# A decoder layer's layernorms: reciprocal roots by a power on GpSimd in place of ScalarE's root and VectorE's reciprocal

## The chip, the cores and the metric

The kernel runs on one core of a Trainium2 chip. A core has five engines with a queue each: TensorE (PE in the profile; PEld are its weight loads), VectorE (DVE), ScalarE (ACT), GpSimd (POOL) and SyncE (SP), which here only issues DMAs. Each engine works its queue in order; semaphores order them among each other. The metric is the device time of one execution in microseconds (us); lower is better.

## The reference

One transformer decoder layer in float32 on x of 4 batches x 1024 tokens x 256 features, with a context of 64 tokens for each batch:

```python
x = x + self_attention(layernorm(x))            # 16 heads of 16, scores not scaled
x = x + cross_attention(layernorm(x), context)  # 16 heads of 16
x = x + ffn(layernorm(x))
# layernorm(v) = (v - mean(v)) / sqrt(var(v) + 1e-5), over the last axis
# ffn(v): h = gelu(v @ ternary(W_fc).T)          # 256 -> 1024
#         h = layernorm(h) * ln_w + ln_b
#         h @ ternary(W_proj).T                  # 1024 -> 256
```

So each batch goes through four layernorms: three over the 256 features of x, and one over the 1024 features inside the feed-forward network (FFN).

## The kernel before

Tokens lie on the 128 partitions; a batch is 8 tiles of 128 tokens. The work has three stretches.

**Start (to about 60 us).** The first batch's layernorm (`ln1(0)`), its projections and loads. Here `state["pinned"]` is true: VectorE's layernorm instructions are held in the order in which the program gives them.

**Attention loop (about 60 to 1090 us).** 16 units (4 batches x 4 head groups) of 16 steps. A step computes scores (TensorE, with the row maxima subtracted by a matmul on `sel`), four exps of 128x512 on ScalarE (L911), the row maxima of the next unit on VectorE (`mx`, L449), and eight weighing matmuls into `ps_acc`. PSUM banks come from a ring of seven. Everything else is written as generators that yield between pieces, and three lines (`due`, `later`, `aside`) with credits decide at which step a piece is put in: the next batches' first layernorm, projections and values; for a finished batch `post(b)`, that is its output projection, the second layernorm, the whole cross-attention, and the statistics of the third layernorm, whose results are kept in `mv3` and `rs3` until the FFN needs them.

**FFN (from about 1087 us).** Eight halves of 512 tokens. `widen(i)` normalises x, multiplies by W_fc, applies Gelu (L1031) and takes the statistics of h (L1034, L1035); after the fourth tile it takes the reciprocal root (`ln_rstd`), then normalises h (VectorE L1042, ScalarE L1045, two tiles each). `narrow(i)` transposes h, splits it into `hT` (ScalarE, L1065) and `hl` (VectorE, L1066) and multiplies by W_proj. The pieces of the wide and narrow halves and of the last batch's `post(3)` are interleaved by a list of places (`WIDE`, `NARROW`) and by tags that a generator yields ("Gelu", "Sqrt", "free Exp").

**A layernorm's steps.** `ln_stats` gives mean and variance of each tile (`mv`; VectorE, L241 and L242). `ln_rstd` makes 1/sqrt(var + eps) for 4 or 8 tiles at once: a root on ScalarE (`sd`, L247) and a reciprocal on VectorE (`rs`, L248). `ln_normalised`, in the attention loop, makes `nmr` = -mean x rs on VectorE (L254) and then eight ScalarE instructions of 128x256 (`xn`, L258); outside it works on VectorE (L265). In the FFN `nmr` is L1039.

**What sets the order.** The matmuls, transposes and SyncE's DMAs are held in program order. The other instructions of VectorE, ScalarE and GpSimd are placed by the framework's scheduler, by its own estimate of when each will be ready; once placed, a queue runs in that order and an instruction that waits holds up what stands behind it. ScalarE's functions come from a table that is loaded by an instruction of its own (ACT_TABLE_LOAD), which the compiler puts in where the function needs another table; the root's, Exp's and Gelu's tables differ, and plain copies and Identity need no load.

GpSimd does little after the start: the copies that pack `xwk` and `xwq` for the cross-attention (L479), two widening copies (L545, L777), and the additions of the output biases to x in the attention loop (`add_row`, L291).

Of the kernel before, what the change touches and what calls it, by code (L numbers as in the profile page):

```python
# [9 lines left out]
F32 = mybir.dt.float32  # L10
F32R = mybir.dt.float32r
DRAM = bass.MemoryType.DRAM
AF = mybir.ActivationFunctionType
ALU = mybir.AluOpType
# [7 lines left out]
P = 128  # L22
NT = S // P
NG = 4
NU = B * NG
LN_EPS = 1e-5
# [4 lines left out]
def decoder_layer(ctx, tc, a, out):  # L31
# [15 lines left out]
    nc = tc.nc  # L47

    const = ctx.enter_context(tc.tile_pool(name="const", bufs=1))
    main_stack = ExitStack()  # L50
    main = main_stack.enter_context(tc.tile_pool(name="main", bufs=1))


    ordered = tc.keep_in_program_order

    def matmul(*args, **kwargs):
        ordered(nc.tensor.matmul(*args, **kwargs))  # L57
# [55 lines left out]
    for name in ("bq", "bk"):  # L113

        t = const.tile([P, 2], F32, name=f"{name}_c")
        for g in range(NG):
            r = 64 * (g % 2)
            dma(
                out=t[r : r + 64, g // 2 : g // 2 + 1],
                in_=a[name].rearrange("(j e) g -> g j e", e=32)[g, :, 1 : 1 + D],  # L120
# [5 lines left out]
    make_identity(nc, ident)  # L126
    eps_t = const.tile([P, 1], F32, name="eps_t")
    nc.vector.memset(eps_t, LN_EPS)

    kx = const.tile([P, 2, B, 4, SK], F32, name="kx")  # L130
    vx = const.tile([P, B, H // 2, 2, 32], F32, name="vx")
# [4 lines left out]
    mv3 = const.tile([P, B * NT, 2], F32, name="mv3")  # L136
    rs3 = const.tile([P, B * NT], F32, name="rs3")
# [6 lines left out]
    post_pool = post_stack.enter_context(tc.tile_pool(name="post", bufs=1, side="right"))  # L144
# [38 lines left out]
    state = {"split": False, "banks": "ring", "pinned": True}  # L183

    def pinned(ins):

        if state["pinned"]:
            ordered(ins)
# [48 lines left out]
    def ln_stats(pool, mv, blocks):  # L237

        for i, t in blocks:
            st = pool.tile([P, 6], F32, tag="bn", name="bn", bufs=3)  # L240
            pinned(nc.vector.bn_stats(out=st, in_=xs(t)[:, 0, :]))  # L241
            pinned(nc.vector.bn_aggr(out=mv[:, i, :], in_=st))  # L242

    def ln_rstd(pool, rs, mv):
        n = mv.shape[1]
        sd = pool.tile([P, n], F32, tag="sd", name="sd", bufs=2)
        nc.scalar.activation(sd, mv[:, :, 1], AF.Sqrt, bias=eps_t[:, 0:1])  # L247
        pinned(nc.vector.reciprocal(out=rs, in_=sd))  # L248

    def ln_normalised(pool, mv, rs, i, t, n):  # L250
        xn = pool.tile([P, n, E], F32, tag="xn", name="xn", bufs=2)
        if state["split"]:
            nmr = pool.tile([P, n], F32, tag="nmr", name="nmr", bufs=2)
            nc.vector.scalar_tensor_tensor(  # L254
                nmr, mv[:, i : i + n, 0], -1.0, rs[:, i : i + n], ALU.mult, ALU.mult
            )
            for k in range(n):
                nc.scalar.activation(  # L258
                    xn[:, k, :], xs(t + k)[:, 0, :], AF.Identity, bias=nmr[:, k : k + 1],
                    scale=rs[:, i + k : i + k + 1],  # L260
                )
            return xn
        for k in range(n):
            pinned(
                nc.vector.tensor_scalar(  # L265
                    xn[:, k, :], xs(t + k)[:, 0, :], mv[:, i + k, 0:1], rs[:, i + k : i + k + 1],
                    ALU.subtract, ALU.mult,
                )
            )
        return xn  # L270
# [64 lines left out]
    def ln1(b):  # L335
        mv = main.tile([P, NT, 2], F32, tag="mv1", name="mv1", bufs=2)
        rs = main.tile([P, NT], F32, tag="rs1", name="rs1", bufs=2)
        xnT_of[b] = xnT = main.tile([P, 2, S], F32, tag="xnT", name="xnT")
        n = NT if state["split"] else NT // 2
        for i0 in range(0, NT, n):  # L340
            for i in range(i0, i0 + n, 2):
                yield "free"
                ln_stats(main, mv, [(i + k, b * NT + i + k) for k in range(2)])
            yield "free"
            ln_rstd(main, rs[:, i0 : i0 + n], mv[:, i0 : i0 + n, :])
            for i in range(i0, i0 + n, 4):
                yield "free"
                xn = ln_normalised(post_pool, mv, rs, i, b * NT + i, 4)
                yield "rows"
                ln_transposed(xnT[:, :, i * P : (i + 4) * P], xn)  # L350
# [205 lines left out]
    def post(b):  # L556
# [15 lines left out]
        mv = post_pool.tile([P, NT, 2], F32, tag="mv2", name="mv2")  # L572
        rs = post_pool.tile([P, NT], F32, tag="rs2", name="rs2")
        for i in range(0, NT, 2):
            yield "free"
            ln_stats(post_pool, mv, [(i + n, t0 + i + n) for n in range(2)])
        yield "free Sqrt"
        ln_rstd(post_pool, rs, mv)
        for half in range(2):
            h0 = half * 4  # L580
            xnT = post_pool.tile([P, 2, 512], F32, tag="xn2T", name="xn2T")
# [76 lines left out]
        sl = slice(t0, t0 + NT)  # L658
        for i in range(0, NT, 2):
            yield "free"  # L660
            ln_stats(post_pool, mv3[:, sl, :], [(i + n, t0 + i + n) for n in range(2)])
        yield "free Sqrt"
        ln_rstd(post_pool, rs3[:, sl], mv3[:, sl, :])
        if b < B - 1:
            dma(out=x_kept[:, sl, :], in_=x_of[b])

# [247 lines left out]
    for u in range(NU):  # L914
# [27 lines left out]
        for step in range(2 * NT):  # L942
# [16 lines left out]
            exps = [scores(u, half, kb, 0)]  # L959
# [42 lines left out]
    ffn = ctx.enter_context(tc.tile_pool(name="ffn", bufs=1))  # L1002
# [4 lines left out]
    def widen(i):  # L1007
        t0 = i * NH
        xh = ffn.tile([P, 2, NH * P], F32R, tag="xh", name="xh", bufs=2)
        xl = ffn.tile([P, 2, NH * P], F32R, tag="xl", name="xl", bufs=2)  # L1010
        for t in range(0, NH, 2):
            cols = slice(t * P, (t + 2) * P)
            xn = ln_normalised(ffn, mv3, rs3, t0 + t, t0 + t, 2)
            ln_transposed(xh[:, :, cols], xn, rest=xl[:, :, cols])
            if t == 0:
                yield ""
        h = ffn.tile([P, NH, HID], F32, tag="h", name="h", bufs=2)
        mv = ffn.tile([P, NH, 2], F32, tag="mvh", name="mvh", bufs=2)
        rs = ffn.tile([P, NH], F32, tag="rsh", name="rsh", bufs=2)
        h_of[i] = h  # L1020
        for t in range(NH):
            yield "Gelu"
            ph = ps["wide"]()
            for half in range(2):
                for k in range(4):
                    c, part = divmod(k, 2)
                    matmul(
                        ph[:, half, :], lhsT=(xl, xh)[part][:, c, t * P : (t + 1) * P],
                        rhs=wfc[:, c, half * 512 : (half + 1) * 512], start=k == 0, stop=k == 3,
                    )  # L1030
            nc.scalar.activation(h[:, t, :], ph.rearrange("p a f -> p (a f)"), AF.Gelu)  # L1031
            st = ffn.tile([P, 2, 6], F32, tag="bnh", name="bnh", bufs=3)
            for half in range(2):
                nc.vector.bn_stats(out=st[:, half, :], in_=h[:, t, half * 512 : (half + 1) * 512])  # L1034
            nc.vector.bn_aggr(out=mv[:, t, :], in_=st)  # L1035
        yield "Sqrt"
        ln_rstd(ffn, rs, mv)
        nmr = ffn.tile([P, NH], F32, tag="nmr", name="nmr", bufs=2)
        nc.vector.scalar_tensor_tensor(nmr, mv[:, :, 0], -1.0, rs, ALU.mult, ALU.mult)  # L1039
        for t in range(0, NH, 2):  # L1040
            yield ""
            nc.vector.tensor_scalar(  # L1042
                h[:, t, :], h[:, t, :], mv[:, t, 0:1], rs[:, t : t + 1], ALU.subtract, ALU.mult
            )
            nc.scalar.activation(  # L1045
                h[:, t + 1, :], h[:, t + 1, :], AF.Identity, bias=nmr[:, t + 1 : t + 2],
                scale=rs[:, t + 1 : t + 2],
            )
# [62 lines left out]
    wides = [Source(widen(i), 16 * i, WIDE) for i in range(halves)]  # L1111
    narrows = [Source(narrow(i), 16 * (i + 1), NARROW) for i in range(halves)]
    exps = turn = 0
    tag = later.tag
    while tag is not None or narrows:
        turn += 1
        if tag is not None and turn % 5 in (0, 2):
            exps += "Exp" in tag
            tag = next(last, None)
            continue  # L1120
        sources = []
        if wides:
            i = halves - len(wides)
            first = len(wides[0].places) <= len(WIDE) - 2
            late_x = i >= 2 * (B - 1) and tag is not None
            full = first and len(narrows) > halves + 1 - i
            apart = exps % NG and tag is not None and wides[0].tag in ("Gelu", "Sqrt")
            if not (late_x or full or apart):
                sources.append(wides[0])
        if narrows and len(narrows) > len(wides):  # L1130
            sources.append(narrows[0])
        if not sources:
            continue
        source = min(sources, key=lambda source: source.places[0])
        source.step()
        if not source:
            (wides if source in wides else narrows).pop(0)
# [58 lines left out]
```

## Time and profile before

| | us |
|---|---|
| three runs | 1352.6, 1344.46, 1348.62 |
| their median | 1348.62 |
| span of the profiled execution, first to last instruction | 1348.4 |
| TensorE, weight loads, VectorE busy | 1277.8, 718.3, 1012.5 |
| ScalarE, GpSimd busy | 896.7, 57.3 |
| mean granted TensorE clock | 0.983 |

The page gives no other time of the profiled execution than its span, which lies 0.2 us below the median. The profile counts as busy what an engine executes; the ends of matmuls are modelled, so a busy TensorE may also be one that goes slowly. A group's line gives the line of the program, engine, operation, output and inputs, shapes and count, then busy time in us and the mean of one in ns, then the idle time just before and who ended it. A timeline's line starts with the start and the duration in us; an idle time before it and its releaser stand in brackets. Granted clock is 1 at full speed and 0.5 when halved.

### The profile page before, as it was taken

What the parts mean: (1) busy time and instruction counts of PE and PEld (TensorE: products, weight loads), DVE (VectorE), ACT (ScalarE), POOL (GpSimd) and SP (SyncE); (2) the same over time, 40 slices, a digit from 0 to 9 for tenths busy, and PEclk for the clock granted to TensorE, in tenths of its full rate; (3) what the DMA queues carried; (4) which work ended last, traced back from release to release, by engine and by line L of the source; (5) the groups of instructions that cost most, each with busy time, mean ns of one, the idle gap of its engine ahead of it and who ended that gap; (6) DMA issues with size and microseconds to landing.
All of it is one profiled execution on the core that took longest, in us unless ns stands there. A gap on an engine that the chain in (4) does not pass through costs nothing.

```text
span 1348.4 us, 27671 instructions
## 1 busy us (share of the span) xinstructions
PE 1277.8 (95%) x11000; PEld 718.3 (53%) x11000; DVE 1012.5 (75%) x2130; ACT 896.7 (67%) x1654; POOL 57.3 (4%) x74
## 2 busy tenths in 40 slices
PE   4889999999999999999999999999999999999887
PEld 2445444545554454444545544545455467676777
DVE  5888877767877877788877777878889369584765
ACT  2377776666677667777676676686766756565854
POOL 5000000021010000011000000010000000000000
PEclk9889999999999999999999999999999999999989
DMA  5442321302020211221111102212210020200000
GB/s 170 122 135 66 93 74 54 96 32 80 33 79 1 64 28 36 70 57 44 53 48 49 44 21 79 80 55 71 55 41 1 1 64 0 64 0 32 1 32 32
DMA packets 46577, 72.73 MB, mean 54 GB/s; under 512 B 11536, under 2 KB 28176, under 8 KB 46448
## 3 DMA queue, kind: packets, MB, share of 16 engines
q1 hardware_dynamic: 45232, 68.73, 17.0%
q8 instruction: 87, 1.43, 0.4%
q0 software_dynamic: 400, 0.66, 0.3%
q10 hardware_dynamic: 816, 1.57, 0.3%
q14 instruction: 42, 0.34, 0.1%
HBM read 46.81 MB, written 24.12 MB: 53 GB/s over the span
## 4 chain that ended last, share of the span: by engine, by line
PE 73%; DVE 16%; ACT 7%; DMA 2%; issue 1%; DVEq 0%; ACTq 0%; SPq 0%
PE ps_ring L57 42%; PE ps_acc L57 15%; PE ps_wide L57 8%; DVE mx L449 8%; PE ps_misc L57 3%; DVE nm L605 3%; PE ps_misc L60 3%; ACT exp L911 2%; PE ps_ring L60 2%; ACT xn L258 1%; DVE bn L241 1%; DVE xn L265 1%; DMA x<-in_x 1%; ACT ex L638 1%; DMA kept_q<-hl 1%
## 5 line engine op out<-in xcount | busy, mean ns | idle before, releaser
L449 DVE TENSOR_REDUCE mx<-ps_ring 128x1 f32<-128x512 f32 x1024 | 645.9, 681 | 151.3 <-PE ps_ring L57 150.5
L911 ACT ACTIVATE exp<-ps_ring 128x512 f32<-128x512 f32 x1024 | 549.1, 607 | 180.5 <-PE ps_ring L57 177.1
L57 PE MATMUL ps_ring<-q,k 64*128 64x512 f32 x1024 | 280.0, 475 | 6.7 <-ACT exp L911 5.9
L57 PE MATMUL ps_ring<-k,q 64*128 64x512 f32 x1024 | 263.3, 423 | 16.1 <-DMA k<-kept_k 6.9
L57 PE MATMUL ps_acc<-exp,v_sb 128*32 128x512 f32 x2048 | 274.5, 608 | 0.0
L57 PE MATMUL ps_ring<-mT,sel 64*128 64x512 f32 x1024 | 233.1, 401 | 0.2 <-ACT mT L467 0.2
L57 PEld LDWEIGHTS ps_ring<-q,k 64*128 64x128 f32 x1024 | 115.9, 186 | 197.1 <-ACT exp L911 68.4
L57 PEld LDWEIGHTS ps_ring<-k,q 64*128 64x128 f32 x1024 | 125.6, 186 | 96.6 <-ACT exp L911 42.1
L57 PEld LDWEIGHTS ps_ring<-mT,sel 64*128 64x128 f32 x1024 | 108.4, 187 | 6.4 <-ACT mT L467 0.7
L57 PEld LDWEIGHTS ps_acc<-exp,v_sb 128*32 128x32 f32 x2048 | 40.4, 108 | 67.4 <-issue 65.6
L1066 DVE SCALAR_TENSOR_TENSOR hl<-ps_misc,lnw,hT 128x512 fp32r<-128x512 f32 x64 | 46.6, 733 | 20.0 <-ACT hT L1065 19.8
L1034 DVE BATCH_NORM_STATS2 bnh<-h 128x6 f32<-128x512 f32 x64 | 41.1, 679 | 24.8 <-ACT h L1031 24.8
L57 PE MATMUL ps_wide<-wfc,xl 128*128 128x512 f32 x128 | 56.2, 439 | 3.4 <-DVE xl L281 2.9
L1031 ACT ACTIVATE h<-ps_wide 128x1024 f32<-128x1024 f32 x32 | 32.7, 1025 | 36.9 <-PE ps_wide L57 36.9
L57 PE MATMUL ps_wide<-wproj,hl 128*128 128x256 f32 x256 | 46.7, 305 | 10.6 <-DVE hl L1066 10.5
L57 PE MATMUL ps_wide<-wfc,xh 128*128 128x512 f32 x128 | 53.1, 415 | 0.0
L1065 ACT ACTIVATE hT<-ps_misc,lnw 128x512 fp32r<-128x512 f32 x64 | 42.9, 687 | 15.4 <-PE ps_misc L60 15.3
L241 DVE BATCH_NORM_STATS2 bn<-x 128x6 f32<-128x256 f32 x96 | 38.9, 416 | 6.0 <-DMA x<-in_x 4.3
L57 PEld LDWEIGHTS ps_wide<-wproj,hl 128*128 128x128 f32 x256 | 35.3, 194 | 14.3 <-DVE hl L1066 12.6
L57 PE MATMUL ps_wide<-wproj,hT 128*128 128x256 f32 x256 | 41.9, 287 | 0.0
L421 ACT COPY v_sb<-ps_ring 128x256 f32<-128x256 f32 x32 | 12.1, 377 | 40.1 <-PE ps_ring L57 40.1
L60 PE MATMUL ps_misc<-ident,h 128*128 128x128 f32 x256 | 37.5, 276 | 0.0
(168 smaller groups left out, 1430.1 us busy)
## 6 DMA issues: line engine op xcount, KB each, us to landing
q<-kept_q SPq DMA_DIRECT2D x240, 64.0 KB
k<-kept_k SPq DMA_DIRECT2D x240, 64.0 KB
kept_q<-hl SPq DMA_DIRECT2D x15, 512.0 KB
kept_k<-hl SPq DMA_DIRECT2D x14, 512.0 KB
out<-x SPq DMA_DIRECT2D x16, 256.0 KB
x<-in_x SPq DMA_DIRECT2D x3, 1024.0 KB
x_kept<-x SPq DMA_DIRECT2D x3, 1024.0 KB
x<-x_kept SPq DMA_DIRECT2D x3, 1024.0 KB
```

Source lines behind the costliest of these rows:

```text
L57: ordered(nc.tensor.matmul(*args, **kwargs))
L60: ordered(nc.tensor.transpose(*args))
L241: pinned(nc.vector.bn_stats(out=st, in_=xs(t)[:, 0, :]))
L258: nc.scalar.activation(xn[:, k, :], xs(t + k)[:, 0, :], AF.Identity, bias=nmr[:, k : k + 1], scale=rs[:, i + k : i + k + 1],)
L265: nc.vector.tensor_scalar(xn[:, k, :], xs(t + k)[:, 0, :], mv[:, i + k, 0:1], rs[:, i + k : i + k + 1], ALU.subtract, ALU.mult,)
L449: nc.vector.tensor_reduce(mx[:, t, 2 * pair + n : 2 * pair + n + 1, kh], pm, AX.X, ALU.max)
L605: nc.vector.tensor_reduce(nm[:, t, s, :], pm[s].rearrange("p (h k) -> p h k", k=SK), AX.X, ALU.max, negate=True,)
L911: nc.scalar.activation(ex[:, n, :], pe[n], AF.Exp)
L1031: nc.scalar.activation(h[:, t, :], ph.rearrange("p a f -> p (a f)"), AF.Gelu)
L1034: nc.vector.bn_stats(out=st[:, half, :], in_=h[:, t, half * 512 : (half + 1) * 512])
L1065: nc.scalar.activation(hT, pt, AF.Copy, scale=w)
L1066: nc.vector.scalar_tensor_tensor(hl, pt, w, hT.bitcast(F32), ALU.mult, ALU.subtract)
```

## The change

The reciprocal root of all layernorms but the first batch's first one goes to GpSimd, as two instructions: rs = var + eps, and rs = rs to the power of -0.5, the exponent read from a constant column (`minus_half`) that VectorE sets once at the start. The first batch's keeps the root and the reciprocal. The tag "Sqrt", by which the pieces around a root were placed, is gone: `fill` looks only for "free", "rows", "cols" and "Exp", so the first two of its uses change no order by themselves; the third one is in the FFN's test `apart`, which now holds back only pieces tagged "Gelu".

```diff
+    minus_half = const.tile([P, 1], F32, name="minus_half")
+    nc.vector.memset(minus_half, -0.5)
...
-    def ln_rstd(pool, rs, mv):
+    def ln_rstd(rs, mv):
         n = mv.shape[1]
-        sd = pool.tile([P, n], F32, tag="sd", name="sd", bufs=2)
-        nc.scalar.activation(sd, mv[:, :, 1], AF.Sqrt, bias=eps_t[:, 0:1])
-        pinned(nc.vector.reciprocal(out=rs, in_=sd))
+        if state["pinned"]:
+            sd = main.tile([P, n], F32, tag="sd", name="sd", bufs=2)
+            nc.scalar.activation(sd, mv[:, :, 1], AF.Sqrt, bias=eps_t[:, 0:1])
+            ordered(nc.vector.reciprocal(out=rs, in_=sd))
+            return
+        nc.gpsimd.tensor_scalar(rs, mv[:, :, 1], LN_EPS, None, ALU.add)
+        nc.gpsimd.tensor_tensor(rs, rs, minus_half[:, 0:1].to_broadcast([P, n]), ALU.pow)
...
-        yield "free Sqrt"
-        ln_rstd(post_pool, rs, mv)
+        yield "free"
+        ln_rstd(rs, mv)
...
-        yield "free Sqrt"
-        ln_rstd(post_pool, rs3[:, sl], mv3[:, sl, :])
+        yield "free"
+        ln_rstd(rs3[:, sl], mv3[:, sl, :])
...
-        yield "Sqrt"
-        ln_rstd(ffn, rs, mv)
+        yield ""
+        ln_rstd(rs, mv)
...
-            apart = exps % NG and tag is not None and wides[0].tag in ("Gelu", "Sqrt")
+            apart = exps % NG and tag is not None and wides[0].tag == "Gelu"
```

More of the change, by code (lines that the diff above doesn't have):

```diff
@@ L344, in ln1 @@
             yield "free"
-            ln_rstd(main, rs[:, i0 : i0 + n], mv[:, i0 : i0 + n, :])
+            ln_rstd(rs[:, i0 : i0 + n], mv[:, i0 : i0 + n, :])
             for i in range(i0, i0 + n, 4):
```

## The prediction

> **What bounds the kernel now.** I read the page from its first two parts to the groups, then the timeline around every table load.
>
> ```profile
> PE 1277.8 (95%) x11000; PEld 718.3 (53%) x11000; DVE 1012.5 (75%) x2130; ACT 896.7 (67%) x1654; POOL 57.3 (4%) x74
> ...
> PEclk9889999999999999999999999999999999999989
> ```
>
> TensorE is busy 95% of the span, so what ScalarE and VectorE do counts only where TensorE waits for them. GpSimd has 57 us of work: it has room.
>
> ```profile
> L247 ACT ACT_TABLE_LOAD x19 | 24.4, 1283 | 1.1 <-PEq L1185 0.7
> ...
> L1031 ACT ACT_TABLE_LOAD x12 | 15.4, 1283 | 2.0 <-PE ps_wide L57 1.8
> ...
> L911 ACT ACT_TABLE_LOAD x9 | 11.5, 1283 | 0.8 <-PE ps_ring L57 0.6
> ...
> L291 POOL TENSOR_TENSOR x<-x,bo 128x512 f32<-128x512 f32 x16 | 20.0, 1280 | 239.4 <-DVE nmr L254 207.9 <-DVE bo L551 27.7 <-ACT xn L258 3.8
> ```
>
> These groups (split by shape) show 43 table loads of 1283 ns with three more at L638. ScalarE's function table goes to the root's and back to Exp's or Gelu's around nearly every layernorm. Now what one costs in the attention loop: ScalarE's timeline at the second layernorm of batch 0.
>
> ```profile
> 362.28 1.28 ACT L247 ACT_TABLE_LOAD   x1
> 363.58 0.30 ACT L247 ACTIVATE sd<-mv,eps_t 128x8 f32<-128x8 f32 x1
> 363.90 1.28 ACT L911 ACT_TABLE_LOAD   x1
> 365.19 2.06 ACT L911 ACTIVATE exp<-ps_ring 128x512 f32<-128x512 f32 x4
> ```
>
> ScalarE gives no exp for 2.9 us. What TensorE loses by it is read from its own timeline: each step of the loop ends in eight weighing matmuls,
>
> ```profile
> 363.86 1.07 PE L57 MATMUL ps_acc<-exp,v_sb 128*32 128x512 f32 x8
> ...
> 368.61 1.06 PE L57 MATMUL ps_acc<-exp,v_sb 128*32 128x512 f32 x8
> ```
>
> and steps with the same matmuls can be compared, since undisturbed ones repeat to 0.02 us. The step between these two lasts 4.75; the same matmuls elsewhere (from 110.04) take 3.77. From 358.93 on, four steps last 4.93, 4.75, 3.37 and 5.38 us, and undisturbed 4.62, 3.77, 2.89 and 4.25: 2.9 us lost. I did this for each root in the loop. Lost: first layernorm of batch 1 (at 80 us) 7.4, of batch 2 (161) 1.9, of batch 3 (580) 4.0; second of batches 0, 1, 2 (362, 621, 886) 2.9, 2.8, 2.9; third of batches 0, 1 (564, 832) 1.7 and 1.5. Together 25 us, and not all the table's: eight normalisations of 0.5 us each also stand on ScalarE among the exps.
>
> **What the change removes.** In the built programs' orders ScalarE has 43 table loads before and 9 after: it loses 34 (18 before a root, 16 that went back) and 19 roots: 34 x 1.283 + 19 x 0.30 = 49 us. VectorE loses 19 reciprocals of 0.2 us, 4 us. TensorE's and SyncE's instructions stand in the same order as before. The Trainium skill, "ScalarE: Activation LUTs", section "What ACT_TABLE_LOAD costs", adds a drain of about 1380 ns to each switch, 2.66 us in all; by it ScalarE would be freed of 96 us. The trace disagrees: an exp ends at 161.11, the load starts at 161.13, the root at 162.43, so I use 1.283.
>
> **What it adds.** GpSimd gets 19 additions and 19 powers, 11 pairs on 128x8 and 8 on 128x4. No row shows a power. From below: the add of 128x512 takes 1.28 us, a memset of 128x1 0.10, so eight columns at an add's price come to 0.10 + 8 x 1.18/512 = 0.12 us. From above: the whole 128x512 add, 1.28 us, which is 64 additions' worth for each element; more than that I can't exclude and keep as a rival. I take the upper end, 1.28 (and 0.7 for four columns), because a logarithm and an exponential in a chain are nearer to many additions than to one. Adding 0.12 for the addition and some 0.25 for three handoffs (VectorE to ScalarE took 0.04 at 83.93), the way from the last statistics to the root is L = 1.65 us for 128x8 and 1.1 for 128x4. Before, it was 0.56 at best (83.93 to 84.49), and up to 2.7 behind a load.
>
> The new wait stands on VectorE: in the loop the scaled mean (nmr, L254) now follows the last aggregate directly or nearly so, so VectorE stands still for L, and the maxima (L449) and bias splits (L371) behind it free PSUM banks late. On ScalarE the first normalisations stand ahead of the next exps and wait too.
>
> **Attention loop, term by term.**
> - Third layernorms of batches 0 and 1: nobody needs the root for long, so all of it goes: 1.7 + 1.5 = **+3.2 us**.
> - Second layernorms (three): ScalarE waits for the root from 362.26 to about 363.9 instead of standing in loads to 365.19, 1.3 us less; but VectorE waits 1.65 it did not wait before, and the normalisations now come in a denser bunch (three and two between pairs of exps). I take 0.9 each: **+2.7**.
> - First layernorm of batch 2: **+0.7** of 1.9; of batch 3: ScalarE gets to its normalisations at 581.3 instead of 583.75, **+1.7** of 4.0.
> - First layernorm of batch 1: **-3.0**. There the load lay beside VectorE's statistics (ScalarE waited until 83.96 anyway), so nothing is won. And GpSimd's queue has a new order: the addition and the power stand ahead of the eight copies of xwk (L479). These ran at 78.82 and TensorE took them at 80.27; now they wait for the statistics' end (83.93) + 1.65 + eight copies at 0.19 = 87.1. TensorE, in order, stands from 80.2 to 87.1 instead of from 82.7 to 86.7, and kx (L518) and the maxima behind it on VectorE come some 4 us later. Against that the load back to Exp (88.29) goes: net -3.
>
> Sum of the loop: **5.3 us**.
>
> **The FFN's end.** From 1087 us on, eight halves each end in a root that their normalisation (L1042, L1045) waits for. From last statistics to first use: 2.5, 1.45, 3.1, 2.9, 2.2, 3.2, 1.35, 1.35 us; after, about 1.35 each. It counts where TensorE stands: 2.9 us at 1114, 1.5 at 1254, 2.7 at 1279, 2.9 at 1303, 1.5 at 1328. Take 1303, on ScalarE's timeline, then TensorE's:
>
> ```profile
> 1300.05 1.28 ACT L247 ACT_TABLE_LOAD   x1
> 1301.34 0.30 ACT L247 ACTIVATE sd<-mvh,eps_t 128x4 f32<-128x4 f32 x1
> 1301.55 0.57 ACT L279 CAST xh<-ps_misc 128x512 fp32r<-128x512 f32 x1
> 1302.08 2.37 ACT L1045 ACTIVATE h<-h,nmr,rsh 128x1024 f32<-128x1024 f32 x2
> ```
>
> ```profile
> 1306.36 1.01 PE L57 MATMUL ps_wide<-wproj,hl 128*128 128x256 f32 x3 [2.89 <-DVE hl L1066]
> ```
>
> Here statistics end at 1300.62 and the root comes as late as before; only the two transposed copies (xh) now stand where the load stood, which brings hT and so TensorE's wproj forward 0.6 us. The same reading gives 1.15 at 1114, 0.85 at 1254, 1.85 at 1279, 1.0 at 1328: 5.45 us. A window of 14 us shows a second price (the granted clock is the third number from the right, 0.76):
>
> ```profile
> 1300.00:1314.00 14.00, 11.11 (x57) 9.62 (x55) 7.31 (x14) 7.79 (x10) 0.00 (x0) 0.76 0.11 39
> ```
>
> After such a gap the clock is halved, here for 6.8 us, 3.4 us after the gaps at 1114 and 1279. Half of these 13.6 us is lost. "TensorE: Matmul & The Clock Gate", section "HAM oscillation", of the Trainium skill puts the limit at idle gaps over about 3.4 us; by it nothing would be won back here. The trace throttles after 2.7 to 2.9. I count one window of 3.4 us avoided, 1.7. Loads back to Gelu lie in waits for TensorE (5.07 us at 1311.88) and bring nothing. Sum: **7.2 us**.
>
> **Sum:** 5.3 + 7.2 = 12.5 from the span of 1348.4: 1336 us. The span and the median of the runs (1348.6) agree, so 1336 it is.
>
> **Rivals.**
> 1. *The power is slow and VectorE stands behind it* (slower). Each us more of L costs six loop layernorms 1 us each and five halves about 0.5: 8.5 us. The gain is used up when the power of 128x8 takes 1.28 + 12.5/8.5 = 2.75 us; at 5 us the time is 1336 + 31 = 1367. For: no row bounds it. Against: GpSimd's rows are short, and VectorE is idle 25% of the time. The skill's "GPSIMD Engine Reference", section 2.1, has about 6 us for the first call of newly loaded code; no run here shows it; by it the layernorm at 80 us would lose 6 more, 1342.
> 2. *The loads were hidden* (no change): new order and bunched normalisations give back what the loads took, the clock windows stay, batch 1 loses more: 1346.
> 3. *Larger gain:* power near its lower end (L 0.5: 8.5 x 1.15 = 10 us more) and all clock windows gone: 1322.
> That all 34 loads go is fixed by the program and is no open point.
>
> **Chances.** A measurement here tells 0.5%, 6.7 us, from no change. Forecast (1328 to 1341) 0.45; larger gain 0.15; no change 0.2; slow power 0.2. So faster 0.6, same 0.2, slower 0.2. The range takes in the lower bound of the power and part of rival 1: 1321 to 1358; in my own case 1328 to 1341.
>
> **What would show it.** Right: 9 table loads on ScalarE; steps at the third layernorms of batches 0 and 1 at their undisturbed length; GpSimd's power near 1.3 us; VectorE idle before L254 about 1.6 us, released by GpSimd; TensorE idle near 80 to 87 us on xwk. Wrong: powers over 2.75 us; TensorE idle in the FFN's halves no shorter; more windows of halved clock than now.

## The result, and the profile after

The changed kernel takes **1364.38 us** (median of four runs, 1363.3 to 1365.78); the kernel before, on the same chip, 1348.54 (1344.46 to 1352.6). The ratio is 1.0116, 95% interval 1.01 to 1.0132: some 16 us slower, where 12.5 us faster was forecast. The profiled execution's span is 1362.7 us, 14.3 more than before.

The head of the page and the slices of TensorE's granted clock, of after:

```profile
PE 1279.9 (94%) x11000; PEld 722.2 (53%) x11000; DVE 1009.2 (74%) x2112; ACT 850.5 (62%) x1601; POOL 89.1 (7%) x112
...
PEclk9889999999999999999999999999999999998989
```

What was to go has gone: ScalarE is busy 46.2 us less (896.7 to 850.5) with 53 instructions fewer (34 loads and 19 roots), VectorE 3.3 us less, and 9 table loads are left. TensorE executes the same 11000 matmuls and is busy 2.1 us more; the other 12 us of the longer span are idle time of TensorE. Now the price that no row of before had, the groups on GpSimd by shape, in the trace of after (count, then busy us and ns of one):

```profile
L254 POOL TENSOR_TENSOR rs<-rs,minus_half 128x8 f32<-128x8 f32 x11 | 18.3, 1666 | 0.9
...
L254 POOL TENSOR_TENSOR rsh<-rsh,minus_half 128x4 f32<-128x4 f32 x8 | 8.3, 1037 | 0.7
```

The power on 128x8 takes 1.67 us, not 1.28, and on 128x4 1.04, not 0.7. Only 0.4 us each: that doesn't explain 28 us between forecast and result.

**Where the time went, in the attention loop.** Steps with the same matmuls were compared, as in the prediction (before to after, lost is plus): first layernorm of batch 1 +0.9, of batch 2 +2.7, of batch 3 -2.1; second layernorms +1.1, +0.6 and +1.1; third layernorm of batch 0 -1.6 and then +2.4, of batch 1 -1.5. With small changes elsewhere the loop is about 3 us longer. Look at one second layernorm, that of batch 0, on VectorE's timeline (start, duration, engine, line, operation; in brackets the idle time before and who ended it). Before:

```profile
361.84 0.18 DVE L242 BATCH_NORM_AGGREGATE mv<-bn 128x2 f32<-128x6 f32 x1
362.30 0.48 DVE L371 SCALAR_TENSOR_TENSOR hl<-ps_ring,bk_c,hl 128x256 f32<-128x256 f32 x1 [0.27 <-ACT hl L370]
362.70 1.28 DVE L449 TENSOR_REDUCE mx<-ps_ring 128x1 f32<-128x512 f32 x2
363.91 0.20 DVE L248 RECIPROCAL rs<-sd 128x8 f32<-128x8 f32 x1
364.03 1.24 DVE L449 TENSOR_REDUCE mx<-ps_ring 128x1 f32<-128x512 f32 x2
365.18 0.22 DVE L254 SCALAR_TENSOR_TENSOR nmr<-mv,rs 128x4 f32<-128x4 f32 x2
```

and after:

```profile
365.56 0.18 DVE L244 BATCH_NORM_AGGREGATE mv<-bn 128x2 f32<-128x6 f32 x1
367.85 0.23 DVE L260 SCALAR_TENSOR_TENSOR nmr<-mv,rs 128x4 f32<-128x4 f32 x2 [2.11 <-POOL rs L254]
368.00 0.48 DVE L377 SCALAR_TENSOR_TENSOR hl<-ps_ring,bk_c,hl 128x256 f32<-128x256 f32 x1
368.39 2.47 DVE L455 TENSOR_REDUCE mx<-ps_ring 128x1 f32<-128x512 f32 x4
```

Before, VectorE split the bias (hl) and took two maxima while ScalarE loaded its table and took the root, and two more before nmr. After, nmr stands first, VectorE does nothing for 2.11 us, and the same hl and the maxima come behind it. What TensorE makes of it, on its timeline of after:

```profile
366.41 0.40 PE L57 MATMUL ps_ring<-mT,sel 64*128 64x512 f32 x2
368.53 0.49 PE L57 MATMUL ps_ring<-k,q 64*128 64x512 f32 x1 [1.73 <-DVE hl L377]
```

TensorE needs a PSUM bank that hl has to read first, and stands for 1.73 us. A second price follows in after's windows of 4 us (the third number from the right is the granted clock, the first is TensorE's busy time):

```profile
366.00:370.00 4.00, 2.12 (x14) 0.84 (x14) 2.15 (x6) 1.96 (x5) 1.73 (x2) 1.00 0.15 60
370.00:374.00 4.00, 4.00 (x32) 1.91 (x26) 1.35 (x3) 3.59 (x9) 2.61 (x3) 0.57 0.20 75
```

In the four us after the gap the mean granted clock is 0.57. The second layernorm of batch 1 allows an estimate of what this adds. TensorE has the same gap there, and the clock stays at 1.00:

```profile
626.52 0.50 PE L57 MATMUL ps_ring<-k,q 64*128 64x512 f32 x1 [1.75 <-DVE hl L377]
628.00:632.00 4.00, 3.43 (x36) 1.65 (x28) 1.93 (x5) 4.00 (x10) 3.11 (x3) 1.00 0.00 0
```

The loss is 0.6 us here and 1.1 for batches 0 and 2, whose gap is followed by a halved window: some 0.5 us for each such window, in this place. (In the last run below, e14, all three gaps are followed by a halved window, and the three lose alike, 2.0 to 2.2 us.) In all, the clock is halved during 64 us of after's execution and 46 of before's. The 18 us between them are five such windows of 3.4 us, so an estimate from these three layernorms is 2 to 3 us in all, and half of 18, 9, is the most that they can cost.

**In the FFN** after is a further 11 us behind. One place of it, after's timeline (some lines left out):

```profile
1185.87 0.15 DVE L1041 BATCH_NORM_AGGREGATE mvh<-bnh 128x2 f32<-128x12 f32 x1
...
1186.13 1.07 ACT L285 CAST xh<-ps_misc 128x512 fp32r<-128x512 f32 x2 [1.18 <-PE ps_misc L60]
...
1187.57 0.16 DVE L1045 SCALAR_TENSOR_TENSOR nmr<-mvh,rsh 128x4 f32<-128x4 f32 x1 [1.16 <-POOL rsh L254]
1187.65 1.53 DVE L1048 TENSOR_SCALAR h<-h,mvh,rsh 128x1024 f32<-128x1024 f32 x2
...
1189.10 1.28 DVE L287 TENSOR_TENSOR xl<-ps_misc,xh 128x512 fp32r<-128x512 f32 x2
1189.84 0.51 PE L57 MATMUL ps_wide<-wfc,xl 128*128 128x512 f32 x1 [2.43 <-DVE xl L287]
```

The same instructions before, on VectorE:

```profile
1181.30 0.15 DVE L1035 BATCH_NORM_AGGREGATE mvh<-bnh 128x2 f32<-128x12 f32 x1
...
1182.18 0.69 DVE L281 TENSOR_TENSOR xl<-ps_misc,xh 128x512 fp32r<-128x512 f32 x1
...
1184.48 0.15 DVE L1039 SCALAR_TENSOR_TENSOR nmr<-mvh,rsh 128x4 f32<-128x4 f32 x1
1184.55 1.53 DVE L1042 TENSOR_SCALAR h<-h,mvh,rsh 128x1024 f32<-128x1024 f32 x2
```

TensorE waits for xl, the low part of the next half's input. Before, the first xl came 0.7 us behind the aggregate and the normalisation of h followed 2.4 us later, when the root was there. After, nmr and the 1.53 us of h stand ahead of xl, which comes 3.1 us behind the aggregate; TensorE falls 2.3 us further back here. The same pattern returns with attx in xl's place (at 1267, 2.2 us) and, at 1285, with hl: there the wait is that of the last batch's third layernorm, whose normalisation (xn, on VectorE in this stretch) stands ahead of statistics and of the split that TensorE needs:

```profile
1282.99 0.41 DVE L271 TENSOR_SCALAR xn<-x,mv,rs 128x256 f32<-128x256 f32 x1 [2.12 <-POOL rs L254]
1283.32 1.28 DVE L1040 BATCH_NORM_STATS2 bnh<-h 128x6 f32<-128x512 f32 x2
1284.52 0.73 DVE L1072 SCALAR_TENSOR_TENSOR hl<-ps_misc,lnw,hT 128x512 fp32r<-128x512 f32 x1
```

In sum, the waits of VectorE for the power (total us, times, longest), after:

```profile
DVE nmr L260 <- POOL rs L254: 10.9, 6, 2.1
DVE nmr L1045 <- POOL rsh L254: 8.8, 8, 1.5
DVE xn L271 <- POOL rs L254: 4.0, 2, 2.1
```

23.7 us, where VectorE waited 7.0 us for ScalarE's roots before (4.2 for `rs`, 2.8 for `rsh`), beside a span that is 14.3 us longer.

### The profile page after: what moved, and what is told of

Same layout as the page of the kernel before. It is cut to its first block, busy times and chain, and to the rows that moved or that the text cites. A ratio compares the mean times of both kernels' runs of the same rounds, so it can differ in the third digit from the quotient of the medians.

```text
span 1362.7 us, 27635 instructions
## 1 busy us (share of the span) xinstructions
PE 1279.9 (94%) x11000; PEld 722.2 (53%) x11000; DVE 1009.2 (74%) x2112; ACT 850.5 (62%) x1601; POOL 89.1 (7%) x112
## 4 chain that ended last, share of the span: by engine, by line
PE 74%; DVE 18%; ACT 4%; POOL 2%; DMA 2%; issue 1%; POOLq 0%; SPq 0%; DVEq 0%; ACTq 0%
PE ps_ring L57 44%; PE ps_acc L57 16%; DVE mx L455 7%; PE ps_wide L57 7%; DVE nm L611 3%; PE ps_ring L60 2%; PE ps_misc L57 2%; PE ps_misc L60 2%; ACT exp L917 1%; DVE bnh L1040 1%; DVE bn L243 1%; DVE hl L1072 1%; POOL rs L254 1%; DVE xn L271 1%; ACT h L1037 1%
## 5 line engine op out<-in xcount | busy, mean ns | idle before, releaser
L57 PE MATMUL ps_ring<-q,k 64*128 64x512 f32 x1024 | 277.0, 474 | 1.9 <-ACT exp L917 1.1
L1072 DVE SCALAR_TENSOR_TENSOR hl<-ps_misc,lnw,hT 128x512 fp32r<-128x512 f32 x64 | 46.6, 734 | 21.9 <-ACT hT L1071 21.9
L57 PE MATMUL ps_ring<-xnT,wq 128*32 128x256 f32 (+1 forms) x456 | 36.5, 405 | 2.7 <-ACT xnT L285 2.7
```

Of the source, the lines that this page charges most:

```text
L1072: nc.vector.scalar_tensor_tensor(hl, pt, w, hT.bitcast(F32), ALU.mult, ALU.subtract)
```

## The experiments

The first theory was that the power's length, in VectorE's and ScalarE's queues, costs the time. Its rivals: that the loads had been hidden anyway, and that the one place where GpSimd's own queue changed (xwk behind the power, batch 1) costs it. The last group tests a theory that the first runs suggested: not the length of the power but the new place of what waits for it. Comments (#) in the edits below were added for this text, and `...` marks what is left out.

### The power replaced by a short operation

```diff
-        nc.gpsimd.tensor_tensor(rs, rs, minus_half[:, 0:1].to_broadcast([P, n]), ALU.pow)
+        nc.gpsimd.tensor_tensor(rs, rs, minus_half[:, 0:1].to_broadcast([P, n]), ALU.subtract)
```

> The power is replaced by a subtraction of the same operands (so the roots are left out: rs is var + eps + 0.5), and every engine's queue keeps the order of the changed kernel. In the changed kernel VectorE waits 25 us in all for GpSimd's roots, at 18 places, and a subtraction of eight columns should take about 0.15 us instead of 1.66, of four columns 0.15 instead of 1.04: some 19 us less waiting. Theory A (the power's own duration is the loss): TensorE gets nearly all of it back, 1345 us or less, as fast as the kernel before or faster. Theory B (the order that the queues were given is the loss: nmr and h ahead of what TensorE waits for on VectorE, the roots ahead of xwk on GpSimd): at most half comes back, 1353 to 1359 us.

Measured: 1344.24 us, ratio to before 0.9968 (0.9956 to 0.9979). All instructions stand in the same order on every engine as in the changed kernel; only the second GpSimd instruction is shorter, 0.20 us on both shapes:

```profile
L254 POOL TENSOR_TENSOR rs<-rs,minus_half 128x8 f32<-128x8 f32 x11 | 2.2, 200 | 0.9
...
L254 POOL TENSOR_TENSOR rsh<-rsh,minus_half 128x4 f32<-128x4 f32 x8 | 1.6, 200 | 0.7
```

So 1.46 us less per root (0.84 on four columns) is worth 20 us: 14 us for each us, where the prediction's rival had 8.5. But the other half of this result is as important: with a nearly free root the change brings only 4 us, while the prediction's own terms, which have the power at 1.28, would give 12.5 + 8.5 x 1.08 = 22. Something else eats some 18 us. And since the scheduler gives the same order for an operation of 0.20 us and for one of 1.67, it makes no difference between them.

### The two stretches by themselves

`ln_rstd` gets an argument that keeps ScalarE's root; first for all first, second and third layernorms, then for all eight of the FFN, then for all but the third layernorms of batches 0 to 2. (The second and third layernorms of the last batch go with the loop's, though they run during the FFN.)

```diff
-        if state["pinned"]:
+        if state["pinned"] or root is not None:
...
# FFN only: the first, second and third layernorms keep the root
+            ln_rstd(rs[:, i0 : i0 + n], mv[:, i0 : i0 + n, :], main)
...
# loop only: the FFN's keeps it
+        ln_rstd(rs, mv, ffn)
...
# third layernorms only: the others keep it, and the last batch's third
+        ln_rstd(rs3[:, sl], mv3[:, sl, :], None if b < B - 1 else post_pool)
```

> Only the FFN's eight roots are powers on GpSimd; all layernorms of the attention loop and of the last batch's post keep ScalarE's root and VectorE's reciprocal. In the changed kernel's trace 10.8 of the 14.3 us were lost after the loop. If the loss stands where the trace shows it: 1357 to 1360 us. If the FFN lost it only because the third and second layernorms of the last batch (in the same stretch) also moved, or because of what the loop left behind: within 4 us of the kernel before, 1345 to 1352.

Measured: 1357.68 us, ratio 1.0068 (1.0043 to 1.0093).

> The reverse: the first, second and third layernorms are powers, the FFN's eight keep the root. By the trace the loop lost 3.1 us, with +3.5 at batch 1's first layernorm, about +1.1 at each second one and -1.5 at each third one; with the last batch's two in the FFN stretch about 1351 to 1354 us. If the two stretches don't add (rival), the sum of the losses of this and of the FFN-only kernel is not 16 us but differs by more than 4.

Measured: 1354.31 us, ratio 1.0042 (1.0027 to 1.0058). The two losses, 0.68% and 0.42%, add up to 1.10% against 1.16% for both: within the intervals the stretches are independent, and each loses.

> Only the third layernorms of batches 0, 1 and 2, whose results nobody needs for long, are powers. The prediction's one term without a wait: 3.2 us gained in the loop, so 1344 to 1346 us against 1348.5 of the kernel before. If taking ScalarE's loads away is worth nothing there: 1348 to 1349.

Measured: 1347.36 us, ratio 0.9995 (0.9979 to 1.001): no difference that can be told. The steps of its trace show where the surest term went. At batch 0's root 1.60 us are won, at batch 1's 1.51, as forecast. But two steps behind batch 0's, TensorE loses 1.55 again, of which the next step gives back 0.77; in after it loses 2.38. There batch 3's x is awaited, which is loaded into the slot that the save of batch 0's leaves. Before and after, VectorE's first statistics on it:

```profile
573.82 0.76 DVE L241 BATCH_NORM_STATS2 bn<-x 128x6 f32<-128x256 f32 x2 [1.64 <-DMA x<-in_x]
```

```profile
578.71 0.75 DVE L243 BATCH_NORM_STATS2 bn<-x 128x6 f32<-128x256 f32 x2 [3.40 <-DMA x<-in_x]
```

The wait for this load was 1.64 us before, is 2.80 in this run and 3.40 in after: TensorE got there earlier by what the root had cost, and the load did not (issued at 572.59 in after, landed 6.1 us later; in before issued at 567.67, landed 6.1 later). Half of batch 0's gain went into a wait for a DMA. What is left in the steps, some 2.2 us of the 3.2 forecast, is 0.16% of the time, less than the interval can tell from nothing. This run's profiled span isn't shorter than before's because it is 2.8 us behind already at 62 us, up to where the two kernels do the same but for one constant; the ten runs spread over 6.8 us.

### Batch 1's first layernorm

> The changed kernel with the first layernorm of batch 1 back on ScalarE and VectorE (two table loads come back). The prediction held that this one gains nothing from the change and loses by GpSimd's queue, where the power stands ahead of the copies of xwk; measured on the steps it lost 0.7 us in the changed kernel (3.5 in the first step, 2.5 of it given back in the next). If that is all: 1362 to 1364 us. If it loses more further on (the clock was halved earlier): 1359 to 1361.

```diff
-            ln_rstd(rs[:, i0 : i0 + n], mv[:, i0 : i0 + n, :])
+            ln_rstd(rs[:, i0 : i0 + n], mv[:, i0 : i0 + n, :], main if b == 1 else None)
```

Measured: 1365.8 us, ratio 1.0131 (1.0114 to 1.0148), not faster than the changed kernel, against both expectations. Against the changed kernel's trace, the step that waits for xwk won 3.45 us, and the two behind it lost 2.67 and 0.84. With the root on ScalarE the three steps are then still 1.0 us longer than in before's trace, and in e4, which has before's own first layernorm, 1.3 longer. So the 0.9 that after loses here can't be put down to the change.

> The changed kernel with batch 1's first addition pinned behind what the program gives GpSimd before it, so that the copies of xwk and xwq stand ahead of it; the root then waits for the copies of xwq, whose data came at 88.9 us, and ScalarE's normalisations are placed later. If the wait of TensorE for xwk was the loss at 80 us: the two steps there get back to at most 12 us together instead of 16, and the kernel to 1360 to 1362. If it only trades one wait for another: 1363 to 1366.

```diff
-        nc.gpsimd.tensor_scalar(rs, mv[:, :, 1], LN_EPS, None, ALU.add)
+        add = nc.gpsimd.tensor_scalar(rs, mv[:, :, 1], LN_EPS, None, ALU.add)
+        if behind:       # batch 1's first layernorm alone
+            ordered(add)  # stays behind the copies of xwk and xwq
```

Measured: 1363.56 us, ratio 1.0111 (1.0094 to 1.0129): no difference from the changed kernel. The wait that the prediction foresaw is there in after, on GpSimd's timeline,

```profile
84.55 1.68 POOL L254 TENSOR_TENSOR rs<-rs,minus_half 128x8 f32<-128x8 f32 x1
86.20 1.48 POOL L485 COPY xwk<-xwk_in 128x64 f32<-128x64 f32 x8
```

and on TensorE's:

```profile
86.48 2.10 PE L57 MATMUL ps_ring<-ctx_in,xwk 128*32 128x256 f32 x16 [6.13 <-POOL xwk L485]
```

but with xwk ready early (e6) that step is 4.8 us shorter than in the changed kernel's trace and the four behind it lose 3.3 of them again. What is left in the steps, 1.5 us, isn't seen in the time. This rival has fallen: the place in GpSimd's queue isn't what costs 16 us.

### Roots in pieces

Each two tiles' root (each tile's in the FFN) is taken right behind their statistics, to leave only the last piece to wait for. In the FFN nmr is then made one tile at a time, for the two tiles that ScalarE normalises.

```diff
+            ln_rstd(rs[:, i : i + 2], mv[:, i : i + 2, :])   # inside the loop over statistics
-        ln_rstd(rs, mv)
...
+            ln_rstd(rs[:, t : t + 1], mv[:, t : t + 1, :])   # FFN, behind each tile's aggregate
```

> The changed kernel with the roots made piecewise: after each two tiles (one tile in the FFN) their addition and power are put on GpSimd, and in the FFN nmr is made for one tile at a time. A power of two columns should take about 0.72 us and one of one column 0.57 (the two durations 1.66 and 1.04 give 0.41 + 0.156 a column), and all but the last lie beside the statistics of later tiles. VectorE's part of h is placed between the statistics, ahead of the last ones. Theory A (duration of the power after the last statistics): most of the 20 us that the subtraction won comes back: 1344 to 1350. Theory B (order): the new order is another one, and where it puts h away from the end it can win more than the subtraction did: 1335 to 1344. If neither (GpSimd's many small instructions delay the last root): 1355 or more.

Measured: 1346.87 us, ratio 0.9989 (0.9976 to 1.0002). The whole loss is back, from 1.0116 to 0.9989: no difference from the kernel before that can be told. The powers' total grew from 26.6 to 49.9 us, and the last piece shrank:

```profile
L254 POOL TENSOR_TENSOR rs<-rs,minus_half 128x2 f32<-128x2 f32 x44 | 31.4, 714 | 3.7
L254 POOL TENSOR_TENSOR rsh<-rsh,minus_half 128x1 f32<-128x1 f32 x32 | 18.5, 577 | 2.7
```

Yet VectorE waits for GpSimd's roots nearly as long in sum as in after, 21.9 us for 23.7 (the three largest here, and 1.2 for xn):

```profile
DVE h L1054 <- POOL rsh L254: 8.6, 12, 1.3
DVE nmr L260 <- POOL rs L254: 7.0, 6, 1.7
DVE nmr L1049 <- POOL rsh L254: 5.1, 9, 1.0
```

So the sum of these waits doesn't price them. And the run doesn't separate length from order: at batch 0's second layernorm the order is after's and the wait before nmr 1.12 us in place of 2.11, but in the FFN the scheduler made a new order, in which VectorE's part of h no longer stands between the last root and xl (at the place shown above, xl comes 1.4 us behind the aggregate, where after has 3.1).

The same with batch 1's first addition held behind xwk:

```diff
-                    ln_rstd(rs[:, i : i + 2], mv[:, i : i + 2, :])
+                    ln_rstd(rs[:, i : i + 2], mv[:, i : i + 2, :], behind=b == 1 and i == 0)
```

> The piecewise kernel with batch 1's first addition pinned: the copies of xwk and xwq come ahead of the last pair of tiles' root only. As the piecewise kernel, or up to 3 us faster if the wait for xwk is worth something.

Measured: 1346.96 us, ratio 0.9993 (0.9976 to 1.001), no difference, as e6.

### The order of the queues

In the built programs TensorE's and SyncE's instructions stand alike before and after; leaving out roots, reciprocals and loads, 181 of VectorE's 2106 places differ and 131 of ScalarE's 1593. The order in which the program issues them is the same in both, so the dropped tag "Sqrt" has no part in this: the scheduler made the difference. These runs force an order: edges without a semaphore between neighbours, in 29 stretches of VectorE's queue and 15 of ScalarE's.

```diff
+AS_BEFORE = {
+    "DVE": (
+        (359, 242, 243, 244, 246, 245, 247, 248, 249, 364, 373),  # numbers in the program's order; 364 is nmr
...
+def order_as_before(nc, tc):
...
+    for engine, rows in AS_BEFORE.items():
+        for row in rows:
+            for first, then in zip(row, row[1:]):
+                tc.add_manual_dep(
+                    traced[engine][then], traced[engine][first].name,
+                    mybir.DependencyInfo(
+                        mybir.DependencyClass.NoSync, mybir.DependencyReason.DATA
+                    ),
...
```

> The changed kernel with all its powers, but VectorE's and ScalarE's instructions forced into the order of the kernel before (less the roots and reciprocals; one pair of ScalarE's stands swapped): the scaled mean and the normalisation stand behind the maxima, splits and copies that the kernel before did while its root was on the way. Theory A (the power costs because the scheduler put what waits for it ahead of ready work on VectorE's and ScalarE's queues; filled with that work the wait is free): 1336 to 1346 us, and VectorE's waits for GpSimd fall from 25 us to under 10. Theory B (the power's length costs wherever it stands, since the normalisation itself is what TensorE needs next): 1356 to 1364. In between, both have a part.

Measured: **1341.33 us**, ratio 0.9931 (0.9908 to 0.9953). The same powers on GpSimd, of the same length, and the kernel is faster than both others. VectorE at batch 0's second layernorm, with this order:

```profile
362.20 0.18 DVE L244 BATCH_NORM_AGGREGATE mv<-bn 128x2 f32<-128x6 f32 x1
362.65 0.48 DVE L377 SCALAR_TENSOR_TENSOR hl<-ps_ring,bk_c,hl 128x256 f32<-128x256 f32 x1 [0.27 <-ACT hl L376]
363.06 2.47 DVE L455 TENSOR_REDUCE mx<-ps_ring 128x1 f32<-128x512 f32 x4
365.45 0.22 DVE L260 SCALAR_TENSOR_TENSOR nmr<-mv,rs 128x4 f32<-128x4 f32 x2
```

The power runs from 362.79 to 364.45 beside hl and the maxima, and when nmr's turn comes nothing has to be waited for. The waits on GpSimd's root that are left:

```profile
DVE nmr L1045 <- POOL rsh L254: 2.9, 4, 0.9
...
DVE nmr L260 <- POOL rs L254: 2.1, 1, 2.1
DVE xn L271 <- POOL rs L254: 1.2, 1, 1.2
```

6.2 us in place of 23.7.

The same, with the subtraction of the first experiment:

```diff
+    order_as_before(nc, tc)
-        nc.gpsimd.tensor_tensor(rs, rs, minus_half[:, 0:1].to_broadcast([P, n]), ALU.pow)
+        nc.gpsimd.tensor_tensor(rs, rs, minus_half[:, 0:1].to_broadcast([P, n]), ALU.subtract)
```

> The same forced order, with the power replaced by a subtraction (the roots are wrong; 0.20 us in place of 1.67). Theory A: the order is what kept the nearly free root at 1344.2 us instead of the 1326 that my forecast's working would give it, so 1328 to 1338. Theory B: the gain was never there (the loads lay beside other work), so 1341 to 1346 as with the scheduler's own order.

Measured: 1337.96 us, ratio 0.9916 (0.9894 to 0.9938). In this order the power's length is worth 3.4 us by the medians, not 20; the intervals of e9 and this run overlap, so even the 3.4 aren't shown.

The old order with the roots in pieces:

```diff
+    order_as_before(nc, tc)
+            ln_rstd(rs[:, i : i + 2], mv[:, i : i + 2, :])   # inside the loop over statistics
+            ln_rstd(rs[:, t : t + 1], mv[:, t : t + 1, :])   # FFN
```

> The forced order with the roots in pieces (two tiles in the loop, one in the FFN, each right behind its statistics, so that only the last piece, 0.7 or 0.6 us, is waited for). Theory A: between the two above, 1332 to 1342, faster than the kernel before. Theory B: 1345 to 1349, as the pieces with the scheduler's own order.

Measured: 1338.55 us, ratio 0.9912 (0.9891 to 0.9933); its interval overlaps that of e9, so that the pieces bring more isn't shown. (20 of VectorE's places still differ from before.) By the medians it is the fastest of the kernels with real powers; it is faster than the kernel before and the changed one.

One queue at a time:

```diff
 AS_BEFORE = {
     "DVE": (...),
-    "Activation": (...),   # left out in the first run below; "DVE" in the second
 }
```

> The changed kernel with VectorE's order alone forced to that of the kernel before; ScalarE's is the scheduler's own (106 of its 1593 places differ from before). If VectorE's queue carries the loss (nmr, h and xn waiting ahead of maxima, xl, attx and hl): 1338 to 1347 us, next to the 1341.3 of both orders. If ScalarE's carries it (the normalisations ahead of the exps): 1356 to 1364. If both do: about 1350.

Measured: 1344.36 us, ratio 0.9955 (0.9939 to 0.9971).

> The mirror of it: ScalarE's order alone as before, VectorE's the scheduler's own (168 of 2106 places differ). If VectorE's queue carries the loss: 1357 to 1366 us; if ScalarE's: 1338 to 1347; if both: about 1352.

Measured: 1365.45 us, ratio 1.0113 (1.0092 to 1.0135). VectorE's order alone brings 1.0116 down to 0.9955; ScalarE's alone brings nothing. What ScalarE's adds to VectorE's (0.9955 to 0.9931) is within the intervals.

And the mirror: the kernel before, held in the order of after.

```diff
+AS_AFTER = {
+    "DVE": (
...
+    order_as_after(nc, tc)
```

> The kernel before (roots on ScalarE, all table loads) with VectorE's and ScalarE's orders forced to those of the changed kernel (37 of VectorE's 2106 places still differ). If the order costs whatever makes the root: the wait for the root is here 0.6 to 2.9 us in place of the power's 2.2, and nothing fills it: 1360 to 1380 us. If the order costs only together with the power: 1345 to 1353.

Measured: 1374.83 us, ratio 1.0187 (1.017 to 1.0204). The root is ScalarE's again, with all 43 loads, and the new order alone (but for 37 of VectorE's places) makes the old kernel 25 us slower. VectorE's waits for the root rise from 7.0 us to 23.0 (13.8 for `rs`, 9.2 for `rsh`). VectorE at the same layernorm:

```profile
363.29 0.18 DVE L242 BATCH_NORM_AGGREGATE mv<-bn 128x2 f32<-128x6 f32 x1
365.36 0.20 DVE L248 RECIPROCAL rs<-sd 128x8 f32<-128x8 f32 x1 [1.88 <-ACT sd L247]
365.59 0.24 DVE L254 SCALAR_TENSOR_TENSOR nmr<-mv,rs 128x4 f32<-128x4 f32 x2
365.75 0.48 DVE L371 SCALAR_TENSOR_TENSOR hl<-ps_ring,bk_c,hl 128x256 f32<-128x256 f32 x1
```

The stall of after, with another engine's name in the brackets.

### The runs together

Ratios to the kernel before, as given above:

| how the root is made | order of before | order of after |
|---|---|---|
| ScalarE's root | 1 | 1.0187 (e14) |
| power on GpSimd | 0.9931 (e9) | 1.0116 (after) |
| subtraction on GpSimd | 0.9916 (e10) | 0.9968 (e1) |

Down a column: the power in place of the root brings 0.7% in either order, 9 us. Across a row: the order costs 1.9% with the root and 1.85% with the power, 25 us. The change does both: 25 - 9 = 16 us slower, as measured. With a subtraction the order costs 0.5%: it hurts because there is a wait in it.

## Why the prediction was wrong, point by point

Of the 28 us between forecast and result some 18 lie in the FFN (7.2 forecast as gain, 11 lost) and some 8 in the loop (5.3 forecast, 3 lost).

- **What it removes**: right. 34 loads and 19 roots left ScalarE. What the whole change is worth where the order is held was also near, 12.5 us forecast and 9 measured, though not term by term, as below.
- **The power's cost**: chosen at the upper end of its bounds, 1.28 us; it took 1.67, and 1.04 for 0.7. The way from the last statistics to the root, L, was 2.11 us at batch 0's second layernorm for 1.65, and 1.55 at 1186 for 1.1. By the prediction's own price that is 0.46 x 8.5 = 4 us. A mis-sized term, not the main cause.
- **The step that failed: what stands behind the wait.** For the second layernorms the prediction said that "VectorE waits 1.65 it did not wait before" and still took a gain of 0.9 us each. Measured is a loss of 1.1, 0.6 and 1.1: TensorE waits 1.73 us for the hl behind nmr. The term took a wait on VectorE for nearly free, though the prediction itself says that what stands behind it frees PSUM banks late. With the old order (e9) the same layernorms gain 1.3 each. The first layernorm of batch 2 likewise: forecast +0.7, measured -2.7, with the old order +0.8.
- **The FFN's end: wrong in sign**, +7.2 forecast, -11 measured. The working followed ScalarE's timeline (load, copies, normalisation) and took VectorE's order as it was before. Its queue was where the change struck: nmr and 1.53 us of h, or xn, went ahead of xl, attx and hl. With the old order (e9) this stretch gains 3 us, less than half of what was forecast.
- **Third layernorms of batches 0 and 1**: the gains came as forecast, 1.6 and 1.5, for 1.7 and 1.5. That the first of them would end in part in the wait for batch 3's x was not seen: what is late next was not asked here, because "nobody needs the root for long". The steps of batch 3's first layernorm, right behind, gave 2.1 for 1.7 forecast; a part of that is the wait made up again, as in e4.
- **First layernorm of batch 1**: -3.0 forecast. The wait for xwk came as described, 6.1 us, but the steps behind it made up for it: -0.9 in the trace, and with ScalarE's root kept the same steps read -1.0 and -1.3 (e5, e4). No loss by the change is shown.
- **Clock**: one halved window fewer was forecast; the halved time rose from 46 to 64 us. In the old order (e9), with the same powers, it is 45. So this comes with the order's gaps and not with the power as such. What it adds is the estimate above, 2 to 3 us; no run separates it.
- **Rivals**: the one that came true is the first, "VectorE stands behind it". Its price was taken as linear from a gain of 12.5 us, with the turning point at 2.75 us. Measured in the new order, the price is 14 us for each us and the gain with nearly no power is 4, so the turning point lies by estimate near 0.2 + 4/14 = 0.5 us: below the prediction's own value for the power. That price belongs to the order and not to the power (e10). The second, that the loads were hidden, is answered by e9: in the order of before the change brings 9 us.
- "GPSIMD Engine Reference", section 2.1, of the Trainium skill has about 6 us for the first call of newly loaded code. The trace doesn't show that for the power: the first, at 84.55, began 0.09 us behind the addition's end and took 1.68 us, where the mean of the eleven is 1.67.

Settled by runs: the order of VectorE's queue carries the loss (e12, e13, e14). Only argued: why the scheduler chose that order. That it gives the same order for the subtraction makes it likely that it reckons the power as short as one.

## What to carry to other kernels

When an operation moves to another engine, the scheduler may arrange the queue of the engine that waits for it anew, as here: compare the orders of the built programs on every engine, and for each instruction that moved ahead of others ask who needs those others. A wait that is filled with other work cost little here (3.4 us by the medians, e9 against e10). The same waits in front of that work cost more than their length: in after VectorE waits 17.5 us longer for the roots than in e9, and the kernel takes some 25 us more. Price the order and the operation apart, by one run with the operation made nearly free and one with the old order forced. Where a gain frees an engine ahead of a fixed transfer, look for the transfer's landing before counting it.

## What the runs showed of the hardware that was not expected

GpSimd's power costs by the column and has a floor: 0.58, 0.71, 1.04 and 1.67 us for 1, 2, 4 and 8 columns on 128 partitions, close to 0.41 + 0.156 per column, while a subtraction of the same 8 or 4 columns takes 0.20. TensorE's clock was halved behind gaps shorter than those that the prediction had read: a mean of 0.57 in the four us that follow the 1.73 us gap shown above. "TensorE: Matmul & The Clock Gate", section "HAM oscillation", of the Trainium skill puts the limit at some 3.4 us of idle time; here TensorE is idle for 1.88 of the four us ahead of the halved window (busy 2.12 of 4 in the line above), so the measurement decides against it in this place. Nor does the gap's length alone decide: the gap of 1.75 us at batch 1's second layernorm was followed by a clock of 1.00.
